# A one-core conditional-residual kernel: the hand-written order of all engines laid out anew

## The chip, the cores and the metric

The kernel runs on one core of one Trainium2 chip. The metric is the device time of one launch in microseconds (us), the median of three runs. Lower is better. TensorE (PE) does matrix products, VectorE (DVE), ScalarE (ACT) and GpSimd (POOL) work on tiles, SyncE (SP) issues transfers inside the core's memory, and POOL also issues the indirect gathers and scatters to and from HBM.

## The reference

The input x has 16 batches of 512 tokens of 512 numbers in float32. Cut to what matters:

```
h = ln(x, pw_g[pathway], pw_b[pathway]); h = ln(h, cp_g[comp], cp_b[comp])
t = ln(x, tm_g[time], tm_b[time])
m, n, r = x + mlp_ln(memory), x + mlp_ln(noise), x + mlp_ln(resource)   # one row per batch
s = ln(x, ms_g[scale], ms_b[scale])
w = softmax(aw)
cat = concatenate([w0*h, w1*t, w2*m, w3*n, w4*r, w5*s])                 # 3072 wide
x + ln(silu(cat @ int_W1 + int_b1) @ int_W2 + int_b2)
```

The large products are those with int_W1 (3072x512) and int_W2 (512x512), for 8192 tokens.

## The kernel before, in words

The 16 batches are 16 windows, each of four rows (blocks) of 128 tokens. The tokens are gathered in an order of the kernel's own (`tok`), in which rows that share a group's scaled layer 1 weights (`vs`) stand together. A window passes through these stages: gathers (POOL), sums and normalised copies (ACT, DVE), transposes (DVE, line L190) with "spreads" that put the transposed blocks in place (SP, L198, four transfers for a row), layer 1 on PE (products `p` at L392 and L440, token sums `u` at L440), a hidden addition (DVE L460) and silu (ACT L463), transposes and spreads of the hidden tile into `cZ`, layer 2 on PE (L541, L543), and the final norm, residual sum and scatter `out<-yb` (POOL L634).

Layer 2 of a pair p of token blocks (p = 0 or 1) is Strassen's scheme with seven half-width products instead of eight. Piece `q7.w.p.k` is product k (lines L541 for the bias, L543 for two accumulating matmuls, each shown as two passes in the profile). Its results stand in two PSUM banks for each p, `pq_pa` and `pq_pb`, each with two halves of 256 columns: products 1 and 6 share the first half of `pq_pa`, product 2 has the second half of `pq_pa`; 5 and 3 share the first half of `pq_pb`, 7 and 4 the second. Since product 6 is added onto product 1, and 3 onto 5, the first value is copied out in between: `kf` (keep_first, ACT, L552 for `pq_pa`, L554 for `pq_pb`), then added to the other half by `sf` (sum_first, DVE L559, L561), and `ku` (keep_last, ACT L565) copies the first half of `pq_pa` once product 6 is in. `sl` (DVE L570, L572) makes the last sums. The POOL sums `zs` (L520 to L526) prepare the operands of products 3 to 7.

Other pieces that the tables name: `xs.n.j` sums of row j of the next window's x (ACT L339, L340, L341), `tx` its transpose, `sp` and `bd` the scaled weights of a group (ACT L246, DVE L254, run only where the group's tables change, a branch at L237), `f1 fs fv fp f2 fn` the chain that makes h, `m7` half-width layer 1 products, `u1` to `u4` and `r1` to `r5` their sums, `ha`, `hs`, `tz`, `sZ` the hidden addition, silu, transpose and spread, `lq lv lp lb po` the end of a window.

The order of all engines is written by hand in three tables of piece names. ORDER is the head (setup, window 0's inputs, the first layer 1 products). WINDOW is the steady list: it is run for w = 0 to 14, with c = window w, n = w+1, m = w+2 and p = w-1, so that one pass does layer 1 of w together with layer 2 of w-1 and the front of w+1. LAST finishes windows 14 and 15. A piece that is already done is skipped:

```
if name not in done:
    done.add(name)
    piece(name)
```

Each engine executes its own instructions in the order in which the tables issue them, and nothing reorders them; the tile framework adds semaphore waits between engines. It keeps them for a whole PSUM tile, not for a half of it.

Of the kernel before, what the change touches and what calls it, by code (L numbers as in the profile page):

```python
# [18 lines left out]


ORDER = """
    wk.1.2 h2.1 fx dk lt pk bx sz wk.1.1 by kd wu.lX.0.1.0 xs.0.0 xt.0.0 tk tt wk.1.3 wk.2.1 gx.e0.0 xv.0.0
    wu.lX.0.1.8 lw fg lo xs.0.1 fl.2 wm.4 h2.2 gx.e0.1 wu.lX.0.1.1 fl.1 scl he.1 xt.0.1 ax he.2 gx.e0.3 gx.e0.2 ac
    xs.e0.0 se xs.0.2 xs.0.3 pwi gh.0.0 h2.0 dp wu.ex.4.0 wk.1.0 gh.0.2 eh.2 xe.0 fl.0 he.0 cv lh eh.0 dc wu.lX.0.1.2
    gc.0.2 xp.0 xs.e0.1 xm.0 eh.1 wu.lX.0.1.3 cs cg do cp tb nv.0.1 xs.e0.2 wu.lX.0.1.4 nv.0.2 cn ct xs.e0.3 xt.0.3
    f1.0.0 fs.0.0 vt.0.1 wu.lX.0.1.5 gc.0.0 nv.0.0 gx.e1.2 ca cm wk.2.3 vt.0.2 cr xv.0.3 xe.e0 cw gx.e1.0 wu.ex.0.0
    vd.0 vt.0.0 xp.e0 vv.0.2 fv.0.0 f1.0.2 fs.0.2 fv.0.2 rp.0 f2.0.2 gx.e1.1 nv.0.3 fp.0.0 gr.e0.0 wk.2.0 xm.e0
    nv.e0.0 fp.0.2 rc.0 rp.1 wu.lX.0.1.6 wk.2.2 wu.lX.0.1.7 f2.0.0 vv.0.0 gr.e0.1 fn.0.0 ro.0 xt.0.2 xs.e1.1 va.0 rc.1
    fn.0.2 vt.0.3 ht.0.0 gh.0.3 ht.0.2 mt.e0.0 xv.0.1 gh.0.1 vv.0.1 ey.0 xv.0.2 gx.1.0 gc.0.1 xa nv.e0.1 nv.e0.2
    mt.e0.1 ez.0 f1.0.3 xs.e1.0 xs.e1.2 sp.0.0 xe.e1 wu.ex.4.1 gx.1.2 hv.0.2 xp.e1 fs.0.3 f1.0.1 fs.0.1 sp.0.1 nv.e0.3  # L30
    ro.1 gr.e0.3 f2.0.1 lX.0.1 bd.0.0 fv.0.1 ey.1 ea.0 gr.e0.2 xm.e1 gx.1.3 ex.0 fp.0.1 ee.0 mt.e0.2 bd.0.1 gx.1.1
    ez.1 lX.0.0 gr.e1.2 fn.0.1 mt.e0.3 vv.0.3 ex.1 eo.0 nv.e1.0 xs.1.2 lX.0.3 ey.2 xs.1.3 ht.0.1 hv.0.0 lV.0.1 ez.2
    fv.0.3 nv.e1.2 vd.1 ea.3 hv.0.1 mt.e1.2 ea.1 tx.1.2 ey.3 ey.6 sp.0.3 gr.e1.0 gc.0.3 ea.4 ea.2 xs.1.0 lX.0.2 fp.0.3
    ar mt.e1.0 lV.0.0 f2.0.3 ee.1 ex.2 gh.1.3 xs.1.1 eo.1 wm.0 fn.0.3 ht.0.3 ez.3 gr.e1.1 xe.1 bd.0.3 wm.1 nv.e1.1
    xp.1 ee.2 wm.2 f1.1.3 ez.6 wh xm.1 ey.4 tx.1.3 mt.e1.1 gh.1.2 sh.0.1 ex.3 ez.4 eo.2 gc.1.3 ey.5 wm.3 nv.1.2 ea.6
    nv.1.0 fs.1.3 tv.1.2 wl.0 ez.5 ex.4 ea.5 ee.3 ex.5 hv.0.3 eo.3 tx.1.1 gc.1.2 ex.6 ee.6 sp.0.2 fv.1.3 gc.1.0 fp.1.3
    bd.0.2 wl.2 wl.1 nv.1.3 lV.0.2 gx.2.2 ee.5 f1.1.2 ee.4 sh.1.3 wl.4 sh.1.2 eo.5 eo.6 f2.1.3 eo.4 lV.0.3 gh.1.0
    tx.1.0 va.1 sX.1.1 fs.1.2 ga.0.2 fn.1.3 wl.3 ga.0.0 sX.1.2 tv.1.0 sh.0.3 sp.1.0 ga.0.1 nv.1.1 th.1.3 tv.1.1 sp.1.1
    tv.1.3 wq wb lH.0.2 fv.1.2 f1.1.0 fp.1.2 lH.0.0 f2.1.2 sX.1.0 ga.0.3 fn.1.2 lH.0.1 ha.0.0 sV.1.0 sh.0.0 fs.1.0
    ha.0.2 ha.0.1 bd.1.1 gc.1.1 sp.1.3 sV.1.1 hs.0.1 gh.1.1 th.1.2 hs.0.0 lH.0.3 sh.0.2 tz.0.1 sV.1.3 sh.1.0 bd.1.3  # L40
    gx.2.1 ha.0.3 bd.1.0 hs.0.3 hs.0.2 fv.1.0 tz.0.3 tz.0.2 sX.1.3 sp.1.2 tz.0.0 bd.1.2 f1.1.1 fs.1.1 gx.2.3 gx.2.0
    fv.1.1 f2.1.0 sV.1.2 sZ.0.0 fp.1.0 fp.1.1 sZ.0.1 f2.1.1 fn.1.0 sZ.0.2 fn.1.1 sZ.0.3 th.1.0 th.1.1 sH.1.0 wz sh.1.1
    sH.1.3 sH.1.1 sH.1.2
"""
# [1436 lines left out]
```

## Time and profile before

| | us |
|---|---|
| median of 3 runs | 938.56 |
| lowest, highest | 936.71, 940.25 |
| span of the profiled execution | 935.9 |
| first layer 1 product of window 1 that ended a wait (PE) | 146.11 |
| layer 2 of window 14, second half starts (PE) | 906.18 |

The span runs from the first to the last instruction. The profiled execution's own time is not listed beside its span; its span lies 2.7 us under the median of the runs, and that difference is taken as what lies around a span. PE is busy for 909.9 us of the span, DVE for 745.0, POOL for 655.0, ACT for 502.1. The mean granted clock of PE is 0.990 of full speed. In timelines, the first number of a row is its start and the second its length; "idle before" in square brackets names what ended a wait.

### The profile page before, as it was taken

Reading aid. Unit: us, or ns where it says so; the run is one execution under the profiler, and the core shown is the slowest. Engines: PE = TensorE matmul, PEld = TensorE weight load, DVE = VectorE, ACT = ScalarE, POOL = GpSimd, SP = SyncE. Lnnn points to the kernel's source line nnn. Section 1 sums busy time; section 2 is a strip of 40 time slices with the busy share of each in tenths; the row PEclk is TensorE's granted clock in tenths of the full one; section 3 lists DMA queues with packets and bytes.
Section 4 is the critical chain, followed back from the end, with each engine's and each line's share of the span. In section 5 each row is a group of like instructions: output and inputs, shape, how many; then the busy total and the mean of one; then the engine's idle time right before and its main releaser. Section 6 shows DMA issues by size and latency. Waiting matters only on the chain. (4 is left out here: it accounts for less than half of the span.)

```text
span 935.9 us, 13631 instructions
## 1 busy us (share of the span) xinstructions
PE 909.9 (97%) x3711; PEld 649.5 (69%) x3711; DVE 745.0 (80%) x1359; ACT 502.1 (54%) x1211; POOL 655.0 (70%) x705
## 2 busy tenths in 40 slices
PE   7999999999999999999999999999999999999996
PEld 6734444877768786868687786878686777767673
DVE  8756776887879697979788786979798987889575
ACT  5557855446372737564654628274656466473322
POOL 9566577667777777677687777776777777775533
...
GB/s 277 256 183 192 181 226 196 185 238 167 247 170 237 189 209 208 194 207 201 237 181 250 165 240 176 219 208 209 204 195 214 201 234 164 247 166 180 185 46 99
DMA packets 88861, 186.68 MB, mean 199 GB/s; under 512 B 24372, under 2 KB 24372, under 8 KB 88780
## 3 DMA queue, kind: packets, MB, share of 16 engines
...
q8 instruction: 31, 0.51, 0.3%
...
q10 hardware_dynamic: 704, 0.08, 0.1%
...
## 5 line engine op out<-in xcount | busy, mean ns | idle before, releaser
L392 PE MATMUL p<-vs,cV 128*128 128x512 f32 x504 | 226.3, 596 | 4.0 <-ACTq L237 2.3
L392 PEld LDWEIGHTS p<-vs,cV 128*128 128x128 f32 x504 | 95.9, 191 | 108.5 <-issue 89.5
L339 ACT ACTIVATE junk<-pw 128x512 bf16<-128x512 f32 x60 | 37.7, 629 | 175.2 <-DVE pw L336 84.9
L440 PE MATMUL p<-wh__80,cH 128*128 128x256 f32 x480 | 111.1, 379 | 0.0
L164 POOL DMA_INDIRECT xbs<-in_x,tok x64 | 69.2, 1081 | 44.4 <-DVE yb L630 24.7
L440 PEld LDWEIGHTS p<-wh__80,cH 128*128 128x128 f32 x480 | 91.2, 190 | 12.4
L634 POOL DMA_INDIRECT out<-yb,tok x64 | 65.4, 1023 | 41.8 <-issue 29.2
L164 POOL DMA_INDIRECT pw<-in_pw,i_pw x64 | 64.7, 1010 | 39.0 <-DVE rH L190 19.9
L164 POOL DMA_INDIRECT cp<-cp_rows,i_cp x64 | 78.8, 1231 | 17.5 <-issue 12.2
L380 POOL TENSOR_TENSOR xbs<-xbs,rows 128x512 f32<-128x512 f32 x64 | 82.2, 1286 | 1.2
L164 POOL DMA_INDIRECT add<-rows,i_add x64 | 67.0, 1048 | 14.7 <-issue 12.5
L361 POOL TENSOR_TENSOR rsh<-veh,mhalf 128x1 f32<-128x1 f32 x64 | 49.2, 768 | 37.2 <-DVE veh L357 32.4
L365 ACT ACTIVATE pw<-pw,rsh 128x512 f32<-128x512 f32 x64 | 44.8, 717 | 53.8 <-issue 23.7
L463 ACT ACTIVATE add<-add 128x512 f32<-128x512 f32 x64 | 38.5, 626 | 63.8 <-DVE add L460 45.4
L335 DVE SCALAR_TENSOR_TENSOR pw<-xbs,sums,pw 128x512 f32<-128x512 f32 x60 | 53.6, 893 | 18.5 <-DMA pw<-in_pw,i_pw 16.2
L372 DVE SCALAR_TENSOR_TENSOR pw<-pw,sumsh,cp 128x512 f32<-128x512 f32 x60 | 44.5, 748 | 18.7 <-DMA cp<-cp_rows,i_cp 7.8
L190 DVE STREAM_TRANSPOSE rH<-pw 128x512 f32<-128x512 f32 x60 | 41.3, 703 | 20.5 <-ACT pw L365 19.8
L440 PE MATMUL p<-wt,cH 128*128 128x256 f32 x240 | 56.7, 379 | 0.0
L440 PE MATMUL u<-wt,ss 128*128 128x256 f32 x240 | 54.5, 380 | 0.4 <-DVE add L454 0.4
L440 PE MATMUL u<-wt,cX 128*128 128x256 f32 x240 | 54.4, 380 | 0.0
L440 PEld LDWEIGHTS u<-wx__79,cX 128*128 128x128 f32 x240 | 45.6, 190 | 12.6 <-issue 5.0
L440 PE MATMUL u<-wx__79,cX 128*128 128x256 f32 x240 | 54.2, 379 | 0.0
...
## 6 DMA issues: line engine op xcount, KB each, us to landing
cZ<-rZ SPq DMA_DIRECT2D x256, 64.0 KB
...
```

Source lines behind the costliest of these rows:

```text
L164: nc.gpsimd.indirect_dma_start(dst, None, table, bass.IndirectOffsetOnAxis(ap=idx, axis=0), **kw)
L190: nc.vector.transpose(rot[:, :, :, j, :].rearrange("p q c t -> p c q t"), src.rearrange("p (c q t) -> p c q t", c=NC, q=Q))
L335: nc.vector.scalar_tensor_tensor(h, st["xb"][:, j, :], st["sums"][:, 1, j : j + 1], h, ALU.add, ALU.mult)
L339: nc.scalar.activation(junk, x, AF.Identity, accum_out=sums[:, 0, k : k + 1])
L361: nc.gpsimd.tensor_tensor(rs, st.pop(("ve", j)), mhalf[:, :1], ALU.pow)
L365: nc.scalar.mul(pw[:, :D], pw[:, :D], st.pop(("rs", j)))
L372: nc.vector.scalar_tensor_tensor(pw[:, :D], pw[:, :D], st["sh", j][:, 1], cp, ALU.add, ALU.mult)
L380: nc.gpsimd.tensor_add(st["xb"][:, j, :], st["xb"][:, j, :], rows[:, 2, :])
L392: nc.tensor.matmul(st["p1", g], st["c" + blk][:, g, c, :], m[:, c, :], start=(blk == first and c == 0), stop=(blk == last and c == NC - 1) ...
L440: nc.tensor.matmul(dst, m[:, c], at_["half1"][k][:, c], start=(k == 1 and c == 0), stop=(c == NC - 1), skip_group_check=True)
L463: nc.scalar.activation(st["add", g], st["add", g], AF.Silu)
L634: nc.gpsimd.indirect_dma_start(out_rows[j], bass.IndirectOffsetOnAxis(ap=tok[:, j, w : w + 1], axis=0), yb[:, j, :], None)
```

## The change

The three tables hold other orders. No piece is added to a launch or taken out, no function is touched. The lines of the changed kernel stand one lower (L552 becomes L553). The core of the diff, the part of WINDOW that holds layer 2:

```
-    xs.n.0 fs.c.3 sh.c.0 bd.c.3 lV.c.3 fv.c.2 f2.c.2 f2.c.3 sZ.p.2 ga.c.0 sZ.p.0 xs.n.1 q7.p.1.1 fp.c.2 fv.c.3 fn.c.2
-    q7.p.0.1 sZ.p.1 fp.c.3 q7.p.0.2 fn.c.3 sZ.p.3 sp.c.2 th.c.2 th.c.3 xs.n.2 zs.p.0 zs.p.1 bd.c.2 q7.p.0.5 kf.p.0
-    q7.p.1.2 sH.c.0 sf.p.0 gh.n.0 zs.p.2 tx.n.3 kf.p.1 tx.n.0 q7.p.0.6 xs.n.3 zs.p.4 q7.p.0.7 ku.p.0 zs.p.5 q7.p.1.5
-    zs.p.3 xe.n kf.p.2 tx.n.1 xp.n ga.c.1 sf.p.1 sH.c.3 tx.n.2 xm.n kf.p.3 q7.p.0.3 q7.p.1.7 sf.p.2 nv.n.3 q7.p.0.4
...
+    m7.c.0.1 m7.c.1.1 lV.c.0 lV.c.3 xs.n.0 fs.c.3 f2.c.3 fv.c.3 f2.c.2 ga.c.0 sh.c.1 fp.c.2 sZ.p.1 sZ.p.2 sZ.p.0
+    q7.p.1.1 xs.n.1 fn.c.2 q7.p.0.1 fp.c.3 fn.c.3 sZ.p.3 tx.n.0 th.c.2 th.c.3 tx.n.3 vd.n tx.n.1 xs.n.2 kf.p.0
+    sp.c.2 zs.p.0 zs.p.1 q7.p.0.2 q7.p.0.5 sH.c.0 zs.p.2 zs.p.3 zs.p.4 sf.p.0 bd.c.2 q7.p.0.6 ku.p.0 xs.n.3 kf.p.2
+    va.n kf.p.1 q7.p.1.2 q7.p.0.7 zs.p.5 q7.p.1.5 gh.n.0 xe.n sf.p.2 sf.p.1 xp.n ga.c.2 xm.n q7.p.1.7 q7.p.0.3
```

In LAST the first product pair stays together, and piece `e1` (one square root of a constant, which loads ACT's table for it, L588) moves from the middle to just ahead of the last scatter:

```
-    q7.p.1.1 tz.c.3 ha.c.1 q7.p.1.2 hs.c.1 po.p.1 po.p.0 zs.p.5 ha.c.0 zs.p.6 hs.c.0 tz.c.1 tz.c.0 kf.p.2 sf.p.2
-    sZ.c.0 q7.p.1.5 q7.p.1.6 w2 kf.p.3 e1 q7.p.1.7 zs.p.7 ku.p.1 sh.c.3 sf.p.3 sl.p.2 q7.p.1.3 q7.p.1.4 l2.c.0 sl.p.3
...
+    zs.p.0 sh.c.2 ga.c.3
+    ga.c.1 zs.p.1 ga.c.2 zs.p.2 zs.p.3 ga.c.0 th.c.2 th.c.3 lV.c.2 lV.c.3 m7.c.0.1 q7.p.0.1 q7.p.0.2 q7.p.0.5
+    kf.p.0 kf.p.1 sH.c.3 sH.c.2 sH.c.0 sH.c.1 sZ.p.3 sZ.p.2 q7.p.0.7 q7.p.0.6 m7.c.1.4 q7.p.0.3 m7.c.1.2 sf.p.0
...
+    rv.c.2 rv.c.3 yg.c.3 ft.c.2 ft.c.3 po.c.2 e1 po.c.3
```

PE before, in a pass of WINDOW, from the second product group of layer 2 on (a name in square brackets is the semaphore that the instruction waits for, by the engine or queue that raises it: Activation is ACT, Pool is POOL, DMAHW are SP's transfers, DMASW POOL's):

```order
L541 MATMUL pq_0a<-b2r,ident 128x256 [waits PE_49]
L543 MATMUL pq_0a<-w_81,cZ_2027 128x256 [waits DMAHW2_49,DMAHW3_49,DMAHW1_49,DMAHW0_49]
L543 MATMUL pq_0a<-w_81,cZ_2027 128x256 x3
L541 LDWEIGHTS ident
L541 MATMUL pq_0b<-b2r,ident 128x256 [waits PE_49]
L543 MATMUL pq_0b<-w_81,cZ_2027 128x256 [waits DMAHW6_49,DMAHW5_49,DMAHW7_49,DMAHW4_49,Pool_49]
L543 MATMUL pq_0b<-w_81,cZ_2027 128x256
L543 MATMUL pq_1a<-w_81,cZ_2027 128x256 x2
L543 MATMUL pq_0a<-w2t,yb 128x256 [waits DVE_49,Pool_49]
```

PE after, at the same place:

```order
L544 MATMUL pq_0a<-w_81,cZ_2035 128x256
L238 UNCONDITIONAL_BRANCH
L544 MATMUL pq_0a<-w_81,cZ_2035 128x256 [waits Activation_49]
L544 MATMUL pq_0a<-w_81,cZ_2035 128x256
L542 LDWEIGHTS ident
L542 MATMUL pq_0b<-b2r,ident 128x256
L238 UNCONDITIONAL_BRANCH
L544 MATMUL pq_0b<-w_81,cZ_2035 128x256 [waits Pool_49]
L544 MATMUL pq_0b<-w_81,cZ_2035 128x256
L544 MATMUL pq_0a<-w2t,yb 128x256 [waits DVE_49,Pool_49]
L544 MATMUL pq_0a<-w2t,yb 128x256
L544 MATMUL pq_1a<-w_81,cZ_2035 128x256 [waits Activation_49]
```

Products 1 and 2 of `pq_0a` stood together and now have a wait for ACT between them; product 2 of `pq_1a` stood ahead of product 6 of `pq_0a` without any wait, and now stands behind it with a wait for ACT.

ACT before, in the same pass:

```order
L341 ACTIVATE junk,sums<-xbs_90,sums 128x512 [waits Activation_49]
L552 COPY yb<-pq_0a 128x256 [waits DMASW6_49,PE_49]
L554 COPY yb<-pq_0b 128x256 [waits DMASW0_49,PE_49]
L339 ACTIVATE junk,sums<-xbs_90 128x512 [waits DMASW2_49,Activation_49]
L340 ACTIVATE sums<-sums 128x1 [waits Activation_49]
L341 ACTIVATE junk,sums<-xbs_90,sums 128x512 [waits Activation_49]
L565 COPY yb<-pq_0a 128x256 [waits DVE_49,PE_49]
L552 COPY yb<-pq_1a 128x256 [waits DMASW3_49]
L554 COPY yb<-pq_1b 128x256 [waits DMASW6_49,PE_49,Pool_49]
```

ACT after:

```order
L342 ACTIVATE junk,sums<-xbs_90,sums 128x512 [waits Activation_49]
L553 COPY yb<-pq_0a 128x256 [waits PE_49]
L238 COMPARE_AND_BRANCH
L247 ACTIVATE vs_84<-ws,scs 128x512 x4
L238 UNCONDITIONAL_BRANCH
L238 UNCONDITIONAL_BRANCH [waits Activation_49]
L238 UNCONDITIONAL_BRANCH
L566 COPY yb<-pq_0a 128x256 [waits DMASW6_49,DVE_49,PE_49]
L340 ACTIVATE junk,sums<-xbs_90 128x512 [waits DMASW1_49,Activation_49]
L341 ACTIVATE sums<-sums 128x1 [waits Activation_49]
L342 ACTIVATE junk,sums<-xbs_90,sums 128x512 [waits Activation_49]
L553 COPY yb<-pq_1a 128x256 [waits DMASW2_49]
```

The copy of the first half of `pq_1a` moved behind `ku` (the copy of `pq_0a` that needs product 6) and behind the sums of row 3; the copy of `pq_0b` moved from second place to behind them all; the sums of a group's weights (L247, taken or jumped over) came in between.

More of the change, by code (lines that the diff above doesn't have):

```diff
@@ L27 @@
[L27 to L31, printed above, removed]
@@ L42 @@
-    fv.1.1 f2.1.0 sV.1.2 sZ.0.0 fp.1.0 fp.1.1 sZ.0.1 f2.1.1 fn.1.0 sZ.0.2 fn.1.1 sZ.0.3 th.1.0 th.1.1 sH.1.0 wz sh.1.1
-    sH.1.3 sH.1.1 sH.1.2
+    cv lt wk.1.3 h2.0 lw lo pk wk.1.2 se dk bx fx h2.2 ax h2.1 dp by kd cw pwi xs.0.0 xs.0.1 fg xs.0.2 xs.0.3 tt
+    he.0 he.2 xe.0 tk gh.0.0 gh.0.2 xp.0 xm.0 xt.0.3 eh.2 wu.lX.0.1.0 sz eh.0 dc fl.2 nv.0.0 nv.0.1 he.1 xv.0.3
+    scl sp.0.1 wm.4 sp.0.0 gc.0.0 gc.0.2 gx.e0.0 cg f1.0.0 wu.lX.0.1.8 vt.0.0 eh.1 xt.0.2 wu.lX.0.1.1 wu.ex.4.0
+    xs.e0.0 ac wk.1.0 gx.e0.2 gx.e0.1 do lh vd.0 fs.0.0 cs f1.0.2 fl.1 wk.2.3 fv.0.0 fs.0.2 f2.0.0 fv.0.2 gx.e0.3
@@ new lines @@
+    cp gx.e1.1 fp.0.0 fp.0.2 cn tb wu.lX.0.1.2 xt.0.1 ct fl.0 wu.lX.0.1.3 wu.lX.0.1.4 vt.0.1 xs.e0.1 xs.e0.2
+    nv.0.3 nv.0.2 vv.0.1 va.1 vv.0.0 fn.0.0 xs.e0.3 ca cm wu.lX.0.1.5 xt.0.0 vt.0.2 ht.0.0 bd.0.1 wk.2.2 f2.0.2
+    bd.0.0 xe.e0 gx.e1.2 gr.e0.0 gr.e0.1 xp.e0 vd.1 wk.1.1 xm.e0 cr xv.0.0 xv.0.1 nv.e0.0 hv.0.0 rp.0 wu.lX.0.1.6
+    vt.0.3 rp.1 wu.ex.4.1 fn.0.2 xv.0.2 nv.e0.1 mt.e0.0 wk.2.0 ey.0 gh.0.1 wu.ex.0.0 gx.e1.0 xs.e1.1 rc.1 ez.0
+    rc.0 va.0 ht.0.2 gh.0.3 gr.e0.2 gx.1.0 xs.e1.0 nv.e0.2 xa mt.e0.1 wk.2.1 nv.e0.3 xs.e1.2 vv.0.2 vv.0.3 xe.e1
@@ new lines @@
+    f1.0.3 f1.0.1 fs.0.1 mt.e0.2 ro.0 ro.1 ex.0 ey.1 wu.lX.0.1.7 lX.0.0 lX.0.3 ey.2 lX.0.1 gx.1.2 gc.0.1 gx.1.3
+    ea.0 xp.e1 fs.0.3 fv.0.1 xm.e1 f2.0.1 tx.1.2 ee.0 gr.e1.2 fp.0.1 gx.1.1 gr.e0.3 sh.0.0 xs.1.2 fn.0.1 ez.1
+    xs.1.3 nv.e1.2 eo.0 ht.0.1 hv.0.2 fv.0.3 hv.0.1 tx.1.3 mt.e1.2 mt.e0.3 ar xs.1.0 ez.2 ex.1 ey.6 lX.0.2 ey.3
+    ea.1 gc.0.3 gh.1.3 ea.4 gr.e1.0 ea.2 ez.6 xs.1.1 wm.0 nv.e1.0 ez.3 ex.2 lV.0.1 tx.1.0 f2.0.3 xe.1 ee.1 mt.e1.0
+    fp.0.3 gr.e1.1 xp.1 ea.3 wh fn.0.3 nv.e1.1 wm.1 sp.0.3 ey.4 ht.0.3 ee.2 mt.e1.1 xm.1 f1.1.3 hv.0.3 eo.1 eo.2
@@ new lines @@
+    gh.1.2 gc.1.3 sh.0.1 ea.6 ea.5 ex.3 lV.0.0 ey.5 wm.2 sp.0.2 wl.1 wl.4 ez.5 ez.4 wl.0 nv.1.2 wm.3 wl.3 fs.1.3
+    nv.1.3 bd.0.2 bd.0.3 ex.5 ex.6 ex.4 lV.0.2 lV.0.3 ee.6 tx.1.1 ee.3 ee.5 f1.1.2 tv.1.3 fv.1.3 f2.1.3 ee.4
+    tv.1.2 gc.1.2 fp.1.3 sh.0.3 nv.1.1 fs.1.2 nv.1.0 fn.1.3 sp.1.0 sp.1.1 eo.5 eo.6 eo.3 sX.1.3 eo.4 tv.1.1 th.1.3
+    bd.1.0 bd.1.1 tv.1.0 fv.1.2 gc.1.1 gh.1.0 fp.1.2 sp.1.3 sX.1.2 wz f2.1.2 ga.0.1 lH.0.0 gx.2.2 gc.1.0 wb ga.0.0
+    sV.1.1 sX.1.0 fn.1.2 f1.1.0 th.1.2 lH.0.1 lH.0.2 lH.0.3 sX.1.1 sV.1.3 sV.1.2 sV.1.0 gx.2.0 ga.0.2 ga.0.3
@@ new lines @@
+    q7.p.0.4 zs.p.6 sh.c.3 zs.p.7 kf.p.3 nv.n.3 nv.n.1 sf.p.3 r1.c.0 sl.p.0 tv.n.3 sl.p.1 tv.n.1 nv.n.0 lq.p.0
+    m7.c.0.2 sH.c.2 sH.c.1 sH.c.3 gh.n.1 gc.n.1 ga.c.3 ga.c.1 q7.p.1.6 q7.p.1.4 q7.p.1.3 nv.n.2 lq.p.1 ku.p.1
+    tv.n.0 f1.n.0 sl.p.2 tv.n.2 sl.p.3 u1.c.1 u1.c.0 fs.n.0 lV.c.2 lq.p.2 lq.p.3 r1.c.1 u2.c.1 m7.c.1.5 m7.c.0.5
+    lv.p u2.c.0 u3.c.0 lp.p lb.p.0 po.p.0 gc.n.0 m7.c.0.6 m7.c.1.6 m7.c.1.2 sV.n.1 sV.n.3 sV.n.0 sV.n.2 f1.n.1
+    u3.c.1 u4.c.0 r5.c.1 r5.c.0 fv.n.0 r2.c.0 lb.p.1 sX.n.0 sX.n.2 m7.c.0.7 fs.n.1 r2.c.1 lb.p.2 u4.c.1 fv.n.1
@@ new lines @@
+    pr.p.1 pr.p.0 zs.p.5 m7.c.1.7 m7.c.1.3 yg.p.0 r2.c.0 yg.p.1 ft.p.0 ft.p.1 ha.c.0 r3.c.1 ha.c.2 ha.c.3 hs.c.2
+    hs.c.3 hs.c.0 m7.c.0.7 m7.c.0.4 q7.p.1.5 q7.p.1.1 tz.c.2 r3.c.0 tz.c.0 ha.c.1 hs.c.1 kf.p.3 kf.p.2 po.p.1
+    sh.c.0 zs.p.6 sh.c.1 w2 zs.p.7 po.p.0 tz.c.3 tz.c.1 sZ.c.0 q7.p.1.7 q7.p.1.6 ku.p.1 sf.p.3 q7.p.1.3 q7.p.1.4
+    q7.p.1.2 l2.c.0 sl.p.2 sl.p.3 sf.p.2 lq.p.3 lq.p.2 sd.p.2 sd.p.3 yg.p.2 yg.p.3 rv.p.2 ft.p.2 rv.p.3 ft.p.3
+    la.c.0 lq.c.0 sd.c.0 sZ.c.3 sZ.c.1 sZ.c.2 po.p.2 po.p.3 l2.c.3 l2.c.1 l2.c.2 rv.c.0 yg.c.0 ft.c.0 la.c.1
```

46 lines of the change are left out of this document (12 added, 34 removed).

## Prediction

> **What bounds the kernel now.** I read the page's totals first, then the stretches, then PE's waits, and last the timelines of one window on PE and ACT.
>
> ```profile
> span 935.9 us, 13631 instructions
> PE 909.9 (97%) x3711; PEld 649.5 (69%) x3711; DVE 745.0 (80%) x1359; ACT 502.1 (54%) x1211; POOL 655.0 (70%) x705
> ...
> 0.00:146.10 146.10, 132.04 (x619) 73.92 (x620) 105.23 (x229) 91.06 (x214) 99.46 (x148) 0.96 0.70 218
> ...
> 161.64:824.58 662.94, 660.05 (x2654) 493.50 (x2653) 550.06 (x977) 362.54 (x881) 488.46 (x490) 1.00 0.73 206
> ...
> 212.25:262.87 50.62, 50.62 (x205) 38.07 (x204) 41.62 (x75) 27.42 (x68) 37.90 (x38) 1.00 0.75 208
> ```
>
> PE is the bound. From 161.64 to 824.58 us lie 13 passes of the steady list, and PE works for 660.05 of 662.94 us at full clock; a pass without a stall takes 50.62 us and has no idle time at all. 13 x 50.62 is 658.06, so the passes that stall lose 4.9 us together. The head, to 146.10, has 14.06 us of idle PE. So in the steady part every microsecond that PE is made to wait is a microsecond of the kernel, while other engines have room (DVE 41.62 of 50.62, ACT 27.42).
>
> PE's waits between 146 and 906 us, summed by what ended them:
>
> ```profile
> PE p L392 <- ACTq L237: 2.3, 1, 2.3
> PE pq_0a L543 <- DVE yb L559: 1.0, 1, 1.0
> ...
> PE u L440 <- DVE add L454: 0.4, 1, 0.4
> ```
>
> No wait of a product `pq` for an ACT copy is among them: in the old order ACT copies a half of a bank after both of its neighbours are in. One pass, on PE and on ACT:
>
> ```profile
> 466.95 0.28 PE L541 MATMUL pq_1a<-b2r,ident 96*128 96x256 bf16 x1
> 467.06 1.03 PE L543 MATMUL pq_1a<-w,cZ 128*128 128x256 f32 x4
> 468.04 1.89 PE L543 MATMUL pq_0a<-w,cZ 128*128 128x256 f32 x8
> 469.88 1.03 PE L543 MATMUL pq_0b<-w,cZ 128*128 128x256 f32 x4
> 470.75 1.03 PE L543 MATMUL pq_1a<-w,cZ 128*128 128x256 f32 x4
> 471.61 1.03 PE L543 MATMUL pq_0a<-w2t,yb 128*128 128x256 f32 x4
> 472.47 1.03 PE L543 MATMUL pq_0b<-w2t,yb 128*128 128x256 f32 x4
> ...
> 469.97 0.37 ACT L552 COPY yb<-pq_0a 128x256 f32<-128x256 f32 x1 [1.14 <-issue]
> 470.94 0.37 ACT L554 COPY yb<-pq_0b 128x256 f32<-128x256 f32 x1 [0.60 <-PE pq_0b L543]
> 471.21 0.63 ACT L339 ACTIVATE junk<-xbs 128x512 bf16<-128x512 f32 x1
> ...
> 472.93 0.35 ACT L565 COPY yb<-pq_0a 128x256 f32<-128x256 f32 x1
> 473.18 0.38 ACT L552 COPY yb<-pq_1a 128x256 f32<-128x256 f32 x1
> ```
>
> A product of four passes starts 0.86 us before its successor (470.75 to 471.61) and shows an end 1.03 us after its start. The row at 468.04 is products 1 and 2 of `pq_0a` back to back. The copy takes 0.37 us; the sums of one row of x, from 471.21 to the copy at 472.93, 1.72 us; a copy follows another after 0.25 us (472.93 to 473.18).
>
> **The change, part by part.** The steady list runs with layer 2 work in w = 1 to 14, so what it does to a pass counts 14 times.
>
> *The first new wait, A.* PE's list now holds `pq_0a` product 1, then product 2 with a wait for ACT, whose copy L553 reads the first half of the same bank and itself waits for product 1. That a write into one half is held until the copy of the other half is done, and how fast it goes on, is shown once in the old trace, at its end, and the restart after a late sum elsewhere:
>
> ```profile
> 910.23 0.37 ACT L554 COPY yb<-pq_1b 128x256 f32<-128x256 f32 x1 [1.63 <-PE pq_1b L543]
> 910.65 0.51 PEld L543 LDWEIGHTS pq_1b<-w2t,zs 128*128 128x128 f32 x3 [0.33 <-ACT yb L554]
> ...
> 369.95 1.10 PE L543 MATMUL pq_0a<-w2t,yb 128*128 128x256 f32 x4 [1.02 <-DVE yb L559]
> 370.89 1.03 PE L543 MATMUL pq_0b<-w2t,yb 128*128 128x256 f32 x4
> ...
> 371.09 0.37 ACT L565 COPY yb<-pq_0a 128x256 f32<-128x256 f32 x1 [0.22 <-PE pq_0a L543]
> ```
>
> The copy ended at 910.60 and the weight load began at 910.65: 0.05 us. The copy at 371.09 began 0.04 us after the product from 369.95 ended (371.05). The restarted product took 0.94 us to its successor instead of 0.86, so a restart costs 0.08. With product 1 starting at T, its end is T+1.03, the copy runs T+1.07 to T+1.44, product 2 starts at T+1.49 instead of T+0.86: 0.63 us, with the restart 0.71. Behind the waiting product on PE stand all others, so it isn't hidden. It can't be less, because the copy needs product 1; it is more where ACT comes late from the sums of row 2.
>
> *The second, B.* Product 2 of `pq_1a` now stands behind product 6 of `pq_0a` and waits for the copy L553 of `pq_1a`. On ACT that copy stands behind L566 (the copy that needs product 6) and the sums of row 3. With product 6 starting at S: its end S+1.03, 0.04 to the copy, 0.25 until the next instruction, 1.72 of sums, 0.37 of copy, 0.05 to PE: start at S+3.46 instead of S+0.86. That is 2.60, with the restart 2.68 us, and PE's idle gap is 2.43. The products behind it (7, 5) have their copies by then: L555 follows 0.37 later, inside product 2's 0.86.
>
> The scaling of a group's weights (L247) that stands between the copies is hidden where it runs: ACT is idle there anyway until product 6 ends. The spreads of `cZ` now go in the order 1, 2, 0, 3, where `pq_0a` product 1 needs row 0:
>
> ```profile
> 457.51 10.63 SPq L198 DMA_DIRECT2D cZ<-rZ  x16
> ```
>
> 16 transfers in 10.63 us are 2.66 a row, so row 0 is issued that much later, up to 465.5, and must land by 468.04. I take 0.1 us a pass as an estimate, between 0 and 0.5. The transposes of x (DVE) now ahead of `sf` fill DVE's idle time there; POOL's and SP's other moves gain slack from the stalls. I take them at nothing; their bounds are -0.1 and +0.3 us a pass, the size of the short waits above (0.4, single).
>
> Per pass 0.71 + 2.68 + 0.1 = 3.49, times 14: **+48.9 us**. Of the 4.9 us that passes lose now, where a group's tables change and DVE or ACT is late, I take 3 as absorbed by the new stalls (bounds 0 and 4.9): **-3**. In LAST products 1, 2 and 5 stay together; product 7 there waits for the copy of 5 alone, one more A: **+0.7**.
>
> *The clock.* A gap of B's size has been in the old trace:
>
> ```profile
> 140.23 3.60 PE L392 MATMUL p<-wh__80,cH 128*128 128x512 f32 x8
> 146.11 5.37 PE L392 MATMUL p<-vs,cV 128*128 128x512 f32 x8 [2.29 <-ACTq L237]
> ...
> 57.13 1.04 PE L1143 MATMUL hs<-ev,sel 128*32 128x512 f32 x2 [1.49 <-ACT ev L1133]
> ...
> 54.30:57.71 3.41, 1.92 (x9) 0.56 (x8) 0.96 (x3) 3.00 (x9) 1.83 (x2) 1.00 1.01 370
> 143.04:146.46 3.42, 1.14 (x3) 0.30 (x2) 2.41 (x6) 1.78 (x4) 3.10 (x4) 1.00 0.67 192
> 146.46:149.87 3.41, 3.41 (x5) 1.35 (x4) 1.05 (x2) 0.00 (x0) 2.64 (x4) 0.50 0.95 266
> ```
>
> After 2.29 us of idle PE the clock was granted at 0.50 for 3.41 us, and eight passes took 5.37 instead of 3.60: 1.77 us lost. After 1.49 us it stayed at 1.00. If the clock is set by stretches of 3.41 us that run on their own, the stretch with 1.14 busy (2.28 idle) lowered it and the one with 1.92 busy (1.49 idle) did not. A gap of 2.43 at a random place puts at least 2.28 idle into one stretch in (3.41 + 2.43 - 2 x 2.28) / 3.41 = 37% of cases, and at least 1.49 in 84%. I take half, nearer to the lower end, since the 2.28 is nearer to the gap's size: 7 x 1.77 = **+12.4** (bounds 0 and 14 x 1.77 = 24.8).
>
> [...]
>
> *Head and end.* The head's products come in another order. Its clock is slow in one more place:
>
> ```profile
> 35.00:50.00 15.00, 15.00 (x86) 8.64 (x85) 10.26 (x39) 4.63 (x18) 7.46 (x8) 0.66 0.69 219
> ```
>
> 0.34 of 15 us are 5.1 us. The head's idle time is 14.06 us, of which the wait that ends at 146.11 is 2.29 and brought 1.77 of slow clock; it can go, or another such come: -4 to +4, and I take -2, because that wait hung on a branch of ACT (L237) that now stands elsewhere. The end:
>
> ```profile
> 914.24 13.90 PE L475 MATMUL p<-w,cZ 128*128 128x512 f32 x32
> ...
> 910.62 1.28 ACT L588 ACT_TABLE_LOAD   x1
> ```
>
> The last products run 13.90 us without a gap, and the table load of 1.28 now comes when the first root is taken, beside them. I take 0, between -2 and +2.
>
> The sum: 935.9 + 48.9 - 3 + 0.7 + 12.4 - 2 = 992.9 us of span, and with the 2.7 that the median stands above the profiled span **995.6 us**.
>
> **Rivals.** *The clock never falls*: the waits A and B alone, 983.2 us. The 1.49 us gap that left the clock alone speaks for it, the 2.29 us gap against; chance 18%. [...] *It falls at every B*: 983.2 + 24.8 = 1008; for it speaks that A puts another 0.46 us of idle time into the same neighbourhood; chance 15%. *No change*: the copies might have been done when PE arrives, and the pass would stay at 50.62; the time would be 938.6 with the head's -4 to +4. The copy of `pq_0a` can't run ahead of product 6 of that bank, which PE issues right before the wait, so this needs a wait that doesn't bind; 3%. *Faster*: the head. It has 14.06 us of idle PE and 5.1 us of slow clock at most; a head without either would give 938.6 - 19 = 919.6. It decides from the point at which the passes lose less than 19 / 14 = 1.4 us each, that is if B weren't there; with B hidden and A left (9.9 us) and half of the head's gain it would be about 939, with A hidden as well 929. 4%.
>
> **How the numbers follow.** The likeliest case, with the clock falling at some of the gaps, has 60% and gives 995.6; by itself it runs from 984 to 1007. The two neighbours reach from 974 (the clock never, the passes' unknown moves and the head 9 us better) to 1012 (always, and 4 us worse). Some 15% is left outside 974 to 1012, most of it the two last rivals. A measurement here can tell about 0.5% (4.7 us) from no change: faster 0.05, same 0.02, slower 0.93.
>
> **What would show it.** The steady pass (from one bias into `pq_1a` to the next) should be 54.0 us without and about 55.8 with a slow stretch. PE's list of waits should have `pq_0a` for ACT's `yb` L553 near 0.5 us, 14 times, and `pq_1a` for the same line near 2.4 us, 14 times; ACT should show L566, a row of sums and L553 in that order behind each product 6. The clock should show 0.50 for 3.41 us behind a part of the gaps, and the page's line of the clock digits below 9 now and then. I am wrong if the gap before `pq_1a` is far under 2.4 us, or if other waits of more than 0.5 us a pass appear (`cZ` spreads on PE, `sf` before product 6, the token sums `u`), or if the head is off by more than 4 us.

## The result, and the profile after

The changed kernel takes 1065.78 us (median of 4 runs, 1062.90 to 1073.89) against 937.63 for the kernel before (4 runs, 935.19 to 940.25): 1.137 times as long, 95% interval 1.131 to 1.142. The sign was right and the size was not: +128 us measured, +57 predicted, and the time lies outside the range of 974 to 1012. The profiled execution (span 1072.1) is the slowest of the four: its mean clock was 0.948, that of the others 0.954 to 0.959, and their spans were 6 to 11 us shorter, so what follows shows somewhat more slow clock than the median run has.

The page's first lines after:

```profile
span 1072.1 us, 13638 instructions
PE 966.8 (90%) x3711; PEld 667.5 (62%) x3711; DVE 749.1 (70%) x1359; ACT 495.0 (46%) x1211; POOL 641.2 (60%) x705
```

PE does the same number of products in 136 us more span. Where it went, by three stretches, cut at the first bias into `pq_1a` and at the first bias of LAST; of each kernel, columns as in the prediction (length, then busy time of PE, PEld, DVE, ACT, POOL, then the granted clock):

```profile
164.64:1011.95 847.31, 768.51 (x2866) 551.92 (x2865) 600.10 (x1057) 386.95 (x956) 511.18 (x529) 0.95 0.62 173
0.00:164.64 164.64, 150.01 (x660) 81.09 (x660) 115.50 (x241) 94.90 (x222) 108.71 (x155) 0.94 0.68 209
1011.95:1072.10 60.15, 48.23 (x189) 34.52 (x187) 33.51 (x62) 13.11 (x34) 21.32 (x22) 0.93 0.31 89
```

```profile
161.64:875.75 714.11, 711.08 (x2857) 531.17 (x2856) 593.88 (x1055) 388.51 (x940) 520.03 (x523) 1.00 0.73 205
0.00:161.64 161.64, 147.57 (x660) 82.11 (x660) 115.92 (x242) 99.30 (x236) 110.97 (x158) 0.96 0.71 217
875.75:935.90 60.15, 51.30 (x197) 36.26 (x195) 35.22 (x64) 14.29 (x35) 23.98 (x26) 0.96 0.31 90
```

The first fence is after, the second before. The head differs by 3 us, the end by nothing (60.15 both). The 14 passes carry the loss: 847.31 against 714.11, +133.2, of which 3.5 us are eight matmuls that stand ahead of the second cut in the new order (x2866 and x2857); the end has them less and takes as long. Idle PE went from 3.0 to 78.8 us (+75.8). Busy PE went from 711.1 to 768.5 (+57.4), and the clock column says why: 24 stretches of 3.41 us in these passes ran at half clock, 41 us lost (0.95 is rounded from 0.952). With the 3.5 of those matmuls some 13 are left, and they lie around the stalls, 61 instead of 5: by the rows in the prediction, a product shows its end 0.17 us after its successor could have started (1.03 against 0.86), and a restart costs 0.08, together 14 us.

PE's waits in the passes after:

```profile
PE pq_1a L544 <- ACT yb L553: 33.9, 14, 2.4
PE pq_0a L544 <- ACTq L238: 21.6, 12, 3.3
PE p L393 <- DVE vs L255: 6.9, 3, 2.6
PE pq_0a L544 <- DMA cZ<-rZ: 5.3, 7, 2.0
PE pq_0a L544 <- ACT yb L553: 3.6, 2, 2.7
PE u L441 <- DVE add L452: 2.4, 14, 0.2
```

The first line is wait B as forecast: 14 times, 2.42 each. The second and fifth are wait A (where the row names ACTq L238, ACT's branch behind the copy is what the wait is put down to): 25.2 us in 14 passes, 1.8 on average, where 0.46 was forecast. One pass, PE and ACT:

```profile
530.20 1.03 PE L544 MATMUL pq_0a<-w,cZ 128*128 128x256 f32 x4
534.57 2.04 PE L544 MATMUL pq_0a<-w,cZ 128*128 128x256 f32 x4 [3.34 <-ACTq L238]
...
538.20 1.03 PE L544 MATMUL pq_0a<-w2t,yb 128*128 128x256 f32 x4
541.64 2.08 PE L544 MATMUL pq_1a<-w,cZ 128*128 128x256 f32 x4 [2.42 <-ACT yb L553]
...
531.25 1.32 ACT L366 ACTIVATE pw<-pw,rsh 128x512 f32<-128x512 f32 x2
532.48 0.61 ACT L340 ACTIVATE junk<-xbs 128x512 bf16<-128x512 f32 x1
...
534.17 0.35 ACT L553 COPY yb<-pq_0a 128x256 f32<-128x256 f32 x1
539.26 0.37 ACT L566 COPY yb<-pq_0a 128x256 f32<-128x256 f32 x1 [4.74 <-PE pq_0a L544]
...
541.24 0.35 ACT L553 COPY yb<-pq_1a 128x256 f32<-128x256 f32 x1
```

Product 1 of `pq_0a` ended at 531.23, but ACT was still at the scalings of h (L366) and the sums of row 2, and copied only at 534.17. Both stalled products show 2.04 and 2.08 us for what takes 1.03: each stall was followed by half clock (granted clock 0.50 from 534.64 to 538.05 and from 541.47 to 544.88).

### The profile page after: what moved, and what is told of

It reads as the page before. It is cut to its first block, busy times and chain, and to the rows that moved or that the text cites. A ratio compares the mean times of both kernels' runs of the same rounds, so it can differ in the third digit from the quotient of the medians.

```text
span 1072.1 us, 13638 instructions
## 1 busy us (share of the span) xinstructions
PE 966.8 (90%) x3711; PEld 667.5 (62%) x3711; DVE 749.1 (70%) x1359; ACT 495.0 (46%) x1211; POOL 641.2 (60%) x705
## 5 line engine op out<-in xcount | busy, mean ns | idle before, releaser
L393 PE MATMUL p<-vs,cV 128*128 128x512 f32 x504 | 231.4, 605 | 13.0 <-DVE vs L255 6.9
L635 POOL DMA_INDIRECT out<-yb,tok x64 | 70.5, 1102 | 128.2 <-issue 87.5
L441 PE MATMUL p<-wh__80,cH 128*128 128x256 f32 x480 | 114.7, 382 | 0.0
L366 ACT ACTIVATE pw<-pw,rsh 128x512 f32<-128x512 f32 x64 | 43.0, 712 | 125.4 <-POOL rsh L362 123.7
L165 POOL DMA_INDIRECT cp<-cp_rows,i_cp x64 | 67.2, 1050 | 21.0 <-issue 16.8
L165 POOL DMA_INDIRECT add<-rows,i_add x64 | 64.8, 1013 | 22.6 <-issue 15.8
L165 POOL DMA_INDIRECT xbs<-in_x,tok x64 | 63.4, 990 | 22.3 <-issue 16.7
L544 PE MATMUL pq_1a<-w,cZ 128*128 128x256 f32 x120 | 40.0, 464 | 35.8 <-ACT yb L553 33.9
L544 PE MATMUL pq_0a<-w,cZ 128*128 128x256 f32 x120 | 37.4, 441 | 30.5 <-ACTq L238 21.6
L622 POOL TENSOR_TENSOR rsy<-vey,mhalf 128x4 f32<-128x4 f32 (+1 forms) x16 | 21.4, 1341 | 71.2 <-DVE vey L617 71.2
L307 ACT ACTIVATE xm<-xbs,nmx,rsx 128x512 f32<-128x512 f32 x64 | 50.2, 807 | 12.7 <-DVE rV L191 5.6
```

Source lines behind the costliest of these rows:

```text
L165: nc.gpsimd.indirect_dma_start(dst, None, table, bass.IndirectOffsetOnAxis(ap=idx, axis=0), **kw)
L307: nc.scalar.activation(t, st["xb"][:, j, :], AF.Identity, bias=st["nm"][:, j : j + 1], scale=st["rs"][:, j : j + 1])
L366: nc.scalar.mul(pw[:, :D], pw[:, :D], st.pop(("rs", j)))
L393: nc.tensor.matmul(st["p1", g], st["c" + blk][:, g, c, :], m[:, c, :], start=(blk == first and c == 0), stop=(blk == last and c == NC - 1) ...
L441: nc.tensor.matmul(dst, m[:, c], at_["half1"][k][:, c], start=(k == 1 and c == 0), stop=(c == NC - 1), skip_group_check=True)
L544: nc.tensor.matmul(home, st["zp", p][k][:, c], at_["half"][k][:, c], start=False, stop=(c == 1), skip_group_check=True)
```

## The experiments

Each run's "before" is the kernel before, run beside it on the same chip. The tables wrap differently in most of these kernels, and their lines stand as in the changed kernel (L553).

**Wait A alone, in the kernel before.**

```
-    q7.p.0.1 ... q7.p.0.2 ... q7.p.0.5 kf.p.0 q7.p.1.2
+    q7.p.0.1 ... kf.p.0 q7.p.0.2 q7.p.0.5 q7.p.1.2
```

> The kernel before, and in its steady list product 2 of pq_0a issued behind ACT's copy of the first half: wait A alone, with the old front. Theory 1 (A costs 0.71 us a pass where ACT comes on time, and grew to 1.8 us idle in the changed kernel because ACT came late there): gap 0.46 us, 14 x 0.71 = +10, no slow clock, about 948. Rival (A is by itself as large as in the changed kernel): 14 x 2.05 = +29 and slow stretches, 967 or more.

Measured 948.95 against 939.16 (ratio 1.010, 1.002 to 1.019): +9.8, as in the sum, but the interval allows 2 to 18. One usual pass, and the row of PE's list (which puts eleven of the 14 down to this copy):

```profile
474.31 1.13 PE L544 MATMUL pq_0a<-w,cZ 128*128 128x256 f32 x4 [0.46 <-ACT yb L553]
...
PE pq_0a L544 <- ACT yb L553: 10.3, 11, 2.7
```

The wait is 0.46 to 0.54 us in ten passes, and a usual pass takes 51.34 us instead of 50.62: 0.72 more, as forecast (0.71). In the other four it is 1.4 to 2.7 us, so ACT comes late now and then with the old front too. The 14 passes take 12.9 us longer (727.03 against 714.11), and the head of this run was 3 us shorter. No stretch of these passes ran at half clock.

**Wait B alone, in the kernel before.**

```
-    q7.p.0.5 kf.p.0 q7.p.1.2 ... q7.p.0.6 xs.n.3 zs.p.4 q7.p.0.7 ku.p.0 ... kf.p.2
+    q7.p.0.5 kf.p.0 ... q7.p.0.6 zs.p.4 ku.p.0 xs.n.3 kf.p.2 q7.p.1.2 q7.p.0.7
```

> The kernel before, and in its steady list product 2 of pq_1a behind product 6 of pq_0a, with ACT's copies in the order ku, sums of row 3, kf.2: wait B alone. Gap 2.42 us in each of 14 passes, 14 x 2.68 = +37.5. Clock theory (a stretch of 3.41 us with at least 1.86 us of idle PE makes the next one slow, and the stretches run on their own): a gap of 2.42 does so in (3.41 + 2.42 - 3.72) / 3.41 = 62% of cases, 5 to 12 of 14, each costing 1.7: +9 to +20, time 984 to 997. Rival (a gap of that size always slows the clock): +24, 1000. Rival (the clock falls only after a gap that comes with another, as A and B do): 976.

Measured 1003.01 against 939.16 (1.068, 1.060 to 1.076): +63.9. The passes, and PE's waits in them:

```profile
158.36:940.55 782.19, 737.54 (x2857) 540.27 (x2856) 606.06 (x1057) 392.47 (x947) 515.13 (x525) 0.97 0.66 188
```

```profile
PE pq_1a L544 <- ACT yb L553: 33.9, 14, 2.4
PE pq_0a L544 <- DVE yb L560: 3.0, 1, 3.0
PE pq_0a L544 <- POOL yb L525: 2.6, 4, 0.8
```

The gap is again 2.42 in all 14 passes. Twelve stretches at half clock took 20.5 us (0.97 is rounded from 0.974); they stand behind nine of the 14 gaps, and behind two other waits of 2 and 3 us. Behind five gaps of 2.42 us there is none, so the theory that a gap of this size always slows the clock is out, and so is the one that needs A beside B. The 6 us above the expected 984 to 997 have the size of the last two rows (5.6 us): product 6 moved 0.86 us forward, and is sometimes ahead of its operands.

**A short B.**

```
-    q7.p.0.6 zs.p.4 ku.p.0 xs.n.3 kf.p.2 q7.p.1.2 q7.p.0.7
+    q7.p.0.6 zs.p.4 ku.p.0 kf.p.2 xs.n.3 q7.p.1.2 q7.p.0.7
```

> As the run with wait B alone, but with the copy of pq_1a ahead of the sums of row 3, so that the gap is 0.71 us instead of 2.42. Theory: 14 x (0.71 + 0.25) = +13.4 and no slow stretch, about 951; the difference to the other run is 14 x 1.72 = 24 of the sums, and the rest is the clock.

Measured 963.17 against 939.16 (1.026, 1.016 to 1.036): +24, ten more than expected; the gap is 0.7 us in each of 14 passes as designed, and product 6 waits for POOL (3.5 us) and DVE (2.6) as above. Two stretches at half clock (3.4 us) stand behind other waits of 2.4 and 2.6 us; the gap of 0.7 brought none. Against the long B the difference is 40 us, 24 of it the sums (14 x 1.72), the rest the clock (17 us less of it).

**Both waits undone in the changed kernel.**

```
-    kf.p.0 sp.c.2 ... q7.p.0.2 q7.p.0.5 ... q7.p.0.6 ku.p.0 xs.n.3 kf.p.2 va.n kf.p.1 q7.p.1.2 q7.p.0.7
+    q7.p.0.2 ... kf.p.0 sp.c.2 ... q7.p.0.5 q7.p.1.2 ... kf.p.1 xs.n.3 q7.p.0.6 ku.p.0 kf.p.2 va.n q7.p.0.7
```

> The changed kernel with the old order of layer 2's products and copies in the steady list (products 1 and 2 of pq_0a together, product 2 of pq_1a ahead of product 6 of pq_0a, the copies as before); everything else stays as changed. Theory 1 (the two new waits and the slow clock that they bring are the whole of the loss): a pass falls from 60.5 to about 51 us, the slow stretches go, and the time is that of before plus the head's 3 and a few single waits, 940 to 952. Rival (the front of the next window, which makes ACT come late, holds PE by itself): ACT's copy of pq_0a comes at 5.1 us behind the first bias instead of 3.0, so the sum and product 6 come 1.3 to 2 us late in each pass, 14 x 1.5 to 2.3 with the restart: 958 to 972, and more if these gaps slow the clock.

Measured 985.85 against 939.16 (1.050, 1.040 to 1.059): +46.7. Theory 1 is wrong, and the rival's 958 to 972 was too low as well. The passes, and PE's waits in them:

```profile
155.32:921.74 766.42, 734.60 (x2866) 530.56 (x2864) 607.83 (x1057) 387.50 (x957) 520.25 (x530) 1.00 0.68 192
```

```profile
PE p L393 <- DVE vs L255: 8.1, 3, 2.7
PE u L441 <- DVE add L450: 7.4, 8, 2.3
PE pq_0a L544 <- DMA cZ<-rZ: 5.5, 7, 2.6
PE u L441 <- DVE add L452: 2.4, 14, 0.2
PE pq_1a L544 <- DMA cZ<-rZ: 2.4, 5, 1.3
```

A pass takes 54.7 us on average instead of 51.0 with the clock near full (3.4 us lost): many short waits for DVE's weights and half sums and for the spreads, none of them above 2.7 us. The 14 passes take 52.3 us more than in the kernel before, 48.8 without the eight matmuls; the head of this run was 6.3 us shorter. The remaining moves of the change, which the prediction took at nothing, cost as much as A and B without the clock.

These waits cost more than the list shows, since idle time counts only from the end that a product shows (1.03 us behind its start, where its successor can start at 0.86). The wait at L452, 0.17 us, stands in every pass of the changed kernel too:

```profile
501.93 1.89 PE L441 MATMUL p<-wh__80,cH 128*128 128x256 f32 x8
503.99 3.72 PE L441 MATMUL u<-wt,cX 128*128 128x256 f32 x16 [0.17 <-DVE add L452]
507.70 1.99 PE L441 MATMUL p<-wh__80,cH 128*128 128x256 f32 x8
509.53 1.89 PE L441 MATMUL p<-wt,cH 128*128 128x256 f32 x8
511.26 1.89 PE L441 MATMUL p<-wh__80,cH 128*128 128x256 f32 x8
```

Eight passes without a wait take 1.73 us (509.53 to 511.26), here 2.06 and then 1.83; the sixteen between them take 3.71 instead of 3.46. That is 0.68 us, 9.5 in 14 passes. It is a wait like A: layer 1's half-width product 7 writes into the PSUM tile `u`, which DVE first has to read for the half sum r2 (L452). Counted in this way, from start to start, the passes with both waits undone lose 56 us, those of the kernel before 8. About 10 of the 56 are this wait, 10 the half sum L450, 9 `vs`, 11 `cZ`, 3 POOL's z sums and 3 the clock; the rest are single waits and a few tenths here and there.

**Wait B undone, A left.**

```
-    kf.p.0 sp.c.2 ... q7.p.0.6 ku.p.0 xs.n.3 kf.p.2 va.n kf.p.1 q7.p.1.2
+    kf.p.0 kf.p.2 sp.c.2 ... q7.p.0.6 kf.p.1 ku.p.0 xs.n.3 va.n q7.p.1.2
```

> The changed kernel with the copies of pq_1a and pq_0b ahead of the copy that needs product 6 and of the sums of row 3: wait B goes, A stays. Additive: B's 14 x 2.65 = 37 and its 12 slow stretches (20) go, 1066 - 57 = 1009. Rival (other late work shows when B no longer covers it, as in the run without both, where passes stayed at 54.7 us instead of 51): 10 to 25 of it comes back as waits of the token sums u, cZ and the weights vs, 1020 to 1035.

Measured 1022.18 (1.093, 1.089 to 1.097), 44 us under the changed kernel: not the additive 57, but the rival's range. PE's two longest waits:

```profile
PE pq_0a L544 <- ACT yb L553: 32.7, 14, 3.4
PE u L441 <- DVE add L450: 10.4, 13, 0.8
```

Covered waits came out: the half sum L450, which is no wait of the changed kernel, and A itself, which grew from 25.2 to 32.7 us, because with B gone PE comes to it earlier and ACT doesn't.

**Why A grew: the place of the copy on ACT.**

```
-    xs.n.1 fn.c.2 q7.p.0.1 ... xs.n.2 kf.p.0 sp.c.2
+    xs.n.1 q7.p.0.1 kf.p.0 fn.c.2 ... xs.n.2 sp.c.2
```

> The changed kernel with one move on ACT: the copy of pq_0a ahead of the two scalings of h (fn, L366) and the sums of row 2 instead of behind them. If ACT's lateness is what made A grow, the copy is free 2.9 us earlier in each pass and A is 0.46 to 0.7 in all of them: 14 x 1.3 = 18 less idle and about 10 slow stretches fewer (17), 1066 - 35 = 1031. If A waits for something else (a branch of the group's weights), it stays at 1.8 and the time at 1060 to 1070. A new wait is possible: h comes later, so the spreads of h and the products m7 and u on PE may wait.

Two runs, 1055.90 and 1076.74: too far apart for a verdict on the time. The waits of the first are clear:

```profile
PE pq_0a L544 <- DVEq L238: 16.0, 11, 1.5
PE pq_0a L544 <- ACT yb L553: 6.5, 14, 0.5
```

A is now 0.46 in all 14 passes (6.5 in sum): what made it grow was the work ahead of the copy on ACT. The time didn't follow, because product 6 now waits up to 1.5 us for DVE, whose sum (L560) stands behind the transposes of h, and h is as late as before.

**Why ACT is late: the gathers on POOL.** In the pass shown above the first sums of a table row on ACT start 5.1 us ahead of the first bias (524.04 and 529.11); in the pass of the kernel before that the prediction shows, 9.0 us ahead (457.93 and 466.95). The gather of that row was issued 15.0 us ahead of the bias after, 16.5 before. So the gathers of x were moved behind it:

```
-    fp.n.0 gx.m.2 gx.m.3 po.p.2 ... gh.n.3 gx.m.1
+    fp.n.0 po.p.2 ... gh.n.3 gx.m.2 gx.m.3 gx.m.1
```

> The changed kernel with one move on POOL: the gathers of rows 2 and 3 of the window after next (gx.m.2, gx.m.3) behind the two gathers of the next window's table rows (gh.n.2, gh.n.3) instead of ahead. Theory (A grew from 0.46 to 1.8 us idle because the table rows are gathered about 1.5 us later in the pass and behind more traffic, so that the sums on ACT ahead of the copy start late): the first scalar_tensor_tensor of rows 2 comes 1.5 to 3 us earlier, A falls to 0.5 to 0.9 us, 14 x 1 to 1.3 = 14 to 18 less idle time and about 10 slow stretches fewer (17): 1066 - 31 to 35 = about 1033. Rival (ACT is late for another reason, as the order of its own list): no change, 1060 to 1070.

Measured 1047.26 (1.120, 1.116 to 1.124): 18 us better by the times, 16 by the ratios, half of the expectation. The sums of the table row did come 3 us earlier, 8.1 us ahead of the bias (506.14 and 514.21 in one pass), so the place of the gathers does set when they start; but ACT's copy of `pq_0a` came only 1 us earlier, 4.1 us behind that bias (5.1 in the pass above).

```profile
PE pq_1a L544 <- ACT yb L553: 33.9, 14, 2.4
PE pq_0a L544 <- DMA cZ<-rZ: 11.7, 13, 1.9
PE pq_0a L544 <- ACTq L238: 11.1, 12, 1.6
PE pq_1a L544 <- DMA cZ<-rZ: 4.5, 3, 1.6
```

A fell by half (11.1 us and 2.1 more in a row not shown), but the waits for `cZ` grew by 9 us: idle time ahead of `pq_0a` and `pq_1a` hardly changed, and was cut into shorter gaps, which slowed the clock less often (mean clock 0.960 against 0.948). The same with the spread order of before and an earlier half sum r1 (`sZ.p.2 sZ.p.0 sZ.p.1`; `r1.c.0 r1.c.1 sl.p.0`), A and B left in:

> The changed kernel with the same three moves, waits A and B left in. A should fall to about 0.5 to 0.9 us, cZ's waits should go, and the sum r1 was covered anyway: the gathers alone gave 1047, without cZ's 16 us of waits there and their share of slow stretches 1020 to 1030.

Measured 1049.26 (1.124, 1.119 to 1.129): the `cZ` waits went (1.5 us left), and A was 31.8 us. The `cZ` waits of product 1 had lain inside A: in both runs ACT's copy comes some 4 us behind the first bias, and product 2 can't start before it is done, however early product 1 is. ACT itself was held by the second gather in line:

```profile
564.49 0.96 POOL L165 DMA_INDIRECT cp<-cp_rows,i_cp  x1 [0.30 <-issue]
...
569.86 1.40 DVE L373 SCALAR_TENSOR_TENSOR pw<-pw,sumsh,cp 128x512 f32<-128x512 f32 x1 [1.25 <-DMA cp<-cp_rows,i_cp]
```

These rows are 7.0 and 1.6 us ahead of that pass's bias (571.48); in the kernel before `cp` was issued 10.3 us ahead. With all x gathers packed in front instead, and the spreads in the order of before again:

```
-    lb.p.2 u4.c.1 ... r3.c.0 lb.p.3 po.p.1 gx.m.0 fp.n.1 fp.n.0 gx.m.2 gx.m.3 po.p.2 ... gh.n.3 gx.m.1
+    lb.p.2 gx.m.1 u4.c.1 ... r3.c.0 gx.m.0 lb.p.3 po.p.1 gx.m.2 gx.m.3 fp.n.1 fp.n.0 po.p.2 ... gh.n.3
```

> The changed kernel (A and B left in) with the gathers of x for the window after next spread earlier over POOL's idle time (gx.m.1 and gx.m.0 ahead of the last two residual sums, all of them ahead of the powers rsh and of the table gathers), and the spreads of cZ in the order 2, 0, 1, 3. In the runs so far ACT's copy of pq_0a comes 4.9 us behind the first bias (changed kernel), 3.9 to 4.1 with only the pw gathers earlier (then the cp gather, issued 7.0 us ahead of the bias instead of 10.3, landed late), 2.2 to 3.0 in the kernel before. Theory (POOL's chain of gathers sets that): pw and cp gathers 1 and 3 us earlier, the copy at 2.2 to 3.0, A at 0.5 to 1.0, idle time before pq_0a and pq_1a down from 66 us to about 42, half of the slow stretches gone: 1015 to 1030. Rival (the copy stays near 4): 1045 or more.

Measured 1082.02 (1.159, 1.149 to 1.168), worse than the change: the powers `rsh` and with them the table gathers came later still (issue 13.8 us ahead of the bias), A grew to 35 us, and PE waited another 11 us ahead of layer 1's products. It fits the chain of gathers, but the intended test, gathers earlier and all else equal, was not reached; how much of A's growth the gathers make stays open.

**What the 47 us are.** From the run with both waits undone, the pieces of one or more engines in WINDOW were put back into the old order among themselves, while the other engines' lists stayed (first POOL, then POOL and DVE, then ACT too, and last PE alone):

> The run with both waits undone (986 us, passes of 54.7), and in its steady list POOL's pieces (gathers, shifts, z sums, powers, scatters) back in the old order; the other engines keep theirs. Theory (the gathers of the table rows come late on POOL, and everything of the front behind them): most of the 47 us go, 945 to 960. Rival (POOL's order is a small part, DVE's is the large one): 975 to 986.

> As the run with POOL's old order, and DVE's pieces in the old order too. PE's waits there were for DVE in 22 us of the 30 (the first half sums r1 behind the hidden additions, the weights vs, r2): if DVE's order is the large part, 940 to 955; if POOL's alone is enough, the same as that run within 5 us.

> As before, and ACT's pieces in the old order too; PE's and SP's stay as changed. If the orders of the engines around PE were all, 936 to 945; what is left over 938 is PE's own order (layer 1 products) and SP's (spreads).

> The run with both waits undone, and in its steady list PE's pieces in the old order, all other engines as changed. Rival to the front theory: the layer 1 products come in an order (u of block 1 ahead of block 0, m7 products of block 3 ahead) in which PE asks for sums before DVE has them. If that is the large part, 945 to 960; if not, 975 or more, with PE waiting elsewhere for the same late pieces.

Measured 1013.60, 1061.73, 1030.67 and 1044.71, against 941.45: all worse than the 985.85 they started from, where all theories expected better. With POOL's old order PE stood idle 34.7 us ahead of layer 1's products, 14 times; with DVE's added, it waited 37.1 us for the half sum L450 and 34.7 for the token sums L428. Our reading is that lists of two different plans don't fit each other; this way of dividing says nothing on which engine's order is at fault. Then single late pieces (the last of these runs has the spread order and the packed gathers of the run above):

```
-    sZ.p.1 sZ.p.2 sZ.p.0
+    sZ.p.2 sZ.p.0 sZ.p.1
-    r1.c.0 sl.p.0 ... lq.p.3 r1.c.1 u2.c.1
+    r1.c.0 r1.c.1 sl.p.0 ... lq.p.3 u2.c.1
```

> The run with both waits undone (986 us), and the spreads of cZ back in the order 2, 0, 1, 3 instead of 1, 2, 0, 3. PE's waits for cZ there sum to 10.3 us with their restarts over 14 passes. Theory (each late piece has its own small price): those go, 986 - 10 = 976. Rival (the transposes of the hidden tile are late themselves, so the order of the four spreads is no matter): 983 to 988.

> The run with both waits undone, and DVE's sum r1 of block pair 1 moved ahead of the token sums u1. PE's waits for that sum (u for add L450) were 9.3 us: 986 - 9 = 977 if the sum's place on DVE is the cause; 986 if the token sums behind it then make PE wait as long.

> The run with both waits undone, with the spread order, the sum r1 and the two table gathers ahead of the two x gathers, all three. If these are the causes of the remaining 47 us (cZ 10, r1 9, and by the gathers the weights vs 8.6 and part of the single waits): 986 - 28 to 35 = 951 to 958. If the orders only hang together as a whole, as the runs with single engines put back suggest, 970 or more.

> The same two moves in the run with both waits undone (986 us). Theory (POOL's gathers are the cause of most of what is left there): PE's waits for vs, cZ and r1 fall by half, 955 to 970. Rival (that rest has other causes, the places of token sums and hidden additions on DVE): 978 or more.

Measured 983.26, 1003.14, 1004.74 and 1002.74 to 1018.10 (two runs, no verdict on the size), the first three against 934.32 and the last against 932.67. The first is the same as the 985.85 within the noise (1.053 against 1.050 times the kernel before), the others are worse. With the spreads in the old order the `cZ` waits fell from 7.9 to 1.5 us, so the rival's time came but not for its reason: the half sum L450 took more (10.7 us instead of 7.4), and product 5 waited for POOL's z sums instead:

```profile
PE u L441 <- DVE add L450: 10.7, 11, 2.0
PE pq_0b L544 <- POOL cZ L523: 8.3, 10, 1.4
```

With r1 moved forward PE waited 13.4 us for the token sums that had stood ahead of it. So these prices don't add: each late piece covers the next. The waits of the 47 us are known, as listed above; which move made them stays open.

**The head alone.** The kernel before with the changed ORDER.

> The kernel before with the changed head alone (ORDER), steady list and end as before. In the runs so far the first bias of pq_1a stood at 161.6, 158.6, 158.4 and 160.4 us with the old head and at 164.6 and 155.3 with the new. Theory: the two heads differ by the luck of the slow clock only, 0.997 to 1.003 of before. Rival: the new head is 4 us shorter, 0.995, about 934, and would be a version that beats both kernels.

Measured 934.51 against 934.79 (10 and 13 runs; 1.000, 0.998 to 1.003): no difference, and the rival's 0.995 is outside. No version found beats the kernel before.

## Why the prediction was wrong

- **Wait B, right.** 2.43 us of gap forecast, 2.42 measured, in 14 of 14 passes, in the change and alone.
- **Wait A, the size in the change wrong.** The step said that product 2 starts 1.49 us behind product 1, and noted that it would be more "where ACT comes late". It took ACT's time of arrival from the old pass, where the sums ended 0.24 us ahead of product 1's end. With the old front that holds in ten of 14 passes (0.72 us a pass; the near match of +9.8 with 9.9 in the sum is partly luck, since the passes gave 12.9 and the head gave 3 back). It failed in the change, where ACT came up to 2.9 us late: 25.2 us of idle time instead of 6.4. In the last three passes, where a wait for `vs` ahead of layer 2 gave ACT time, A was 0.46.
- **The other moves "at nothing", wrong, the largest miss.** Bounds of -0.1 to +0.3 us a pass were taken from single short waits. Measured with A and B undone: 46.7 us in the time, and in the passes 48.8, 3.5 each. The step looked at each moved piece by itself and gave it the slack of the old pass, and layer 1's new order, with its wait for r2, wasn't looked at. We think that the slack was shared (gathers, sums, scalings, transposes and spreads of the front stand in line, and two or three of them moved at once); no run shows this by itself.
- **"-3 absorbed", wrong.** The passes in which a group's weights change got new waits (`vs`, 6.9 us).
- **The clock, the term mis-sized.** 12.4 forecast for seven stretches, 41 measured for 24 in the profiled run. The stretches were right: 3.41 us long, with borders on a grid and not at the stalls (below). The number of gaps was not: twelve of the stretches stand behind B, nine behind A and the `cZ` waits next to it (A was 1.9 us or more in nine passes), three behind waits for `vs`. And half of B's gaps was too few: 1.88 us of idle time in a stretch was followed by half clock (below), where the step had counted from 2.28. With 1.9 a gap of 2.42 would count in about 60% of places at random, by our estimate, (3.41 + 2.42 - 2 x 1.9) / 3.41; it did in 9 of 14 with B alone and in 12 of 14 in the change.
- **Head, LAST and end**, -2, +0.7 and 0 forecast: in the profiled run +3.0 for the head, and the same 60.15 us for the rest with 3 us less work in it; 0 for the head alone. The 2.7 us taken for what lies around a span are 1.8 in the profiled run after (1073.89 and 1072.1).

The three parts measured apart, +9.8 for A, +63.9 for B with its slow clock, +46.7 for the rest, sum to 120 of the 128 us. That the sum is near is luck, since the parts overlap: A in the change is partly the rest showing through, as the run with the copy first shows, and taking B out of the change gave 44 us, not 64.
